# Four-layer graph network on one core: where the transposed adjacency lies in memory, and when the last pair of layer 2 is finished

## The chip, the cores and the metric

The kernel runs on 1 core of one Trainium2 chip, in float32. The time is the device time of one launch in microseconds (us), median over runs. Engines are called as in the profile: PE (TensorE matmul), DVE (VectorE), ACT (ScalarE), POOL (GpSimd) and SP (SyncE, which here only issues DMAs).

## The reference

`x` has 32 batches of 512 nodes and 64 features; `adj` is a 512 by 512 symmetric, normalized adjacency with self edges. Each of four layers adds its result to x:

```python
# layer 0
h = relu(layernorm(x));  x = x + h @ Ws + (adj @ h) @ Wn + bias
# layer 1, twice: z = relu((adj @ z) @ W[i]), from z = h
h = relu(layernorm(x));  x = x + z
# layer 2: graph attention
h = relu(layernorm(x));  Wh = h @ W.T;  e = leaky_relu(e1[:, None] + e2[None, :], 0.2)
x = x + elu(softmax(where(adj > 0, e, -9e15)) @ Wh)
# layer 3: 8 heads and an output attention, each as
#   s = (h h^T) * adj;  s = where(s == 0, -1e16, s);  softmax(s) @ h + b
# heads joined by leaky_relu, then the output attention and leaky_relu, added to x
```

## The kernel before

**Tiling.** Nodes lie on the 128 partitions, four to each (C = 4), and batches are worked on in 16 pairs. x stays in SBUF for the whole launch. Layers 0 to 2 run as a software pipeline over the pairs (`slot(k)`), in which each pair is a few steps behind the one before it. The tail of that pipeline, `drain()`, is an order written out by hand: the string `LAST` names each step and its pair (`exp_15` is the exp of pair 15, the last).

**Layer 3** is a list `flow` of units: 128 head units (two heads of one batch each) and 16 output units. `flow_period(t)` issues period t of a pipeline over units: the scores of unit t (rows r = 2, 3) and of unit t+1 (r = 0, 1), L428 on PE; their maxima (L443 on DVE: one custom instruction that adds the mask, negates and keeps the row maximum; two for each r, as a unit holds two heads); the row maxima go out to DRAM and come back broadcast (`spread_out`, `spread_in`, on SP's queue) into `topb`; unit t-1 has the maximum subtracted (`shift`, L467 and L471, on POOL in most periods; in period 3, EARLY + 1, rows 1 and 3 are on DVE) and the exp (L480 on ACT); rows are joined in pairs (`join`, L483 on DVE), summed (`totals`), and multiplied with the features (`values`, L489 on PE), after which `normalize` (L538 on DVE) writes `o_att` and so frees the `av` bank. The score tiles have two buffers in PSUM (`ps_s`), which the odd rows' exps also use. The first two units are begun within `drain()`, so that layers 2 and 3 overlap; their `topb` lies in the memory of the transposed adjacency `adj_t`, which by then is read no more (L457). Unit 1's four shifts are on POOL.

**The end of a layer 2 pair.** `read` (L1161) forms o; `exp` (L1169, ACT) its exponential; `grow` (L1175, L1176 and the two instructions of `centre`, L919 and L921) adds elu(o) to x, sums the rows and writes the centred x over o; `square` (L1180, ACT) and a sum (L958, DVE) give the variance; `root` (L965, ACT, a square root, for which ACT loads another function table) and `turn` (L973, DVE, a reciprocal) the factor that layer 3's features of that pair need. Those features are used only when layer 3 comes to batches 30 and 31. The last pair's o and e are kept past layer 2: `o_end` and `e_end` take both buffers of the tag `hs3` in the pool `early`, which layer 3 uses for scaled features (`features(2)`, L575). In the kernel before, `end_of_gat` does grow, square, sum, root and turn of the last pair between periods 2 and 3.

**Memory.** Pools are laid one behind the other. Behind what is kept for good comes `setup` (8 KB for each partition for `adj_raw`, later the mask, and some 4.2 KB of small weights), then `adj_t` (8 KB), then the buffers of layers 0 to 2. After layer 2 all of these are given back, and layer 3's pools take their place: `pairs_b`, five buffers of 4 KB for pairs of rows (cat and y), and then `pbuf`, six buffers of 4 KB for `p_att`, where maxima are written. Five times 4 KB is a little less than the 20.5 KB or so of setup and `adj_t`, so that the first `p_att` buffer begins on the last bytes of `adj_t`, which are the second half of unit 1's `topb`. Unit 2's first maxima go into that buffer.

**Order.** In both stages the order of instructions on PE, DVE and ACT is the order of the source (`manual_schedule`); in layer 3 also that of POOL and SP. Waits between engines are put in where memory or data asks for them.

Of the kernel before, what the change touches and what calls it, by code (L numbers as in the profile page):

```python
# [8 lines left out]
F32 = mybir.dt.float32  # L9
# [5 lines left out]
P = 128  # L15
# [7 lines left out]
def fast_form(  # L23
# [26 lines left out]
    B, N, F = x.shape  # L50
    C = N // P
# [20 lines left out]
    early = ctx.enter_context(tc.tile_pool(name="early", bufs=1))  # L72
# [6 lines left out]
    lasting += [  # L79
        adj_p.rearrange("p c k q -> p c (k q)")[:, c : c + 2] for c in range(0, C, 2)  # L80
    ]
    setup_ctx = ExitStack()
    setup = setup_ctx.enter_context(tc.tile_pool(name="setup", bufs=1))
    adj_raw = setup.tile([P, C, N], F32, name="adj_raw", tag="raw")
# [57 lines left out]
    m2 = const.tile([P, H, F], F32, name="m2")  # L142
    bh01 = const.tile([P, H], F32, name="bh01")
    wa1 = setup.tile([P, P], F32, name="wa1")
    adj_t_ctx = ExitStack()
    adj_t_pool = adj_t_ctx.enter_context(tc.tile_pool(name="adjt", bufs=1))
    adj_t = adj_t_pool.tile([P, C, N], F32, name="adj_t")

    adj_f = adj_p.rearrange("p c k q -> p c (k q)")
    flow_neg = const.tile([P, C, N], F32, name="flow_neg")  # L150

# [98 lines left out]
    def row_pair(name):  # L250

        return pairs.tile([P, 2, N], F32, name=name, tag="row")
# [102 lines left out]
    EARLY = 2  # L355
# [429 lines left out]
    def planned(units, products):  # L785

        class Nothing:
            def __getattr__(self, name):
                return lambda *args: None

        nothing = Nothing()

        def period(t):
            def unit(lag):
                return units[t - lag] if 0 <= t - lag < len(units) else nothing


            now, ahead, last = (unit(i) if t - i >= EARLY else nothing for i in (0, -1, 1))
            made = unit(1) if t > 1 else nothing
            summed = unit(2) if t > 2 else nothing  # L800
            for r in range(2, C):
                now.scores(r)
            unit(3).recips_in()
            unit(6).store()
            unit(4).bias()
            last.shift(0, nc.gpsimd)
            made.exps(0)
            summed.totals()
            summed.totals_out(1, nc.scalar)
            u, h = products.get(t - 1, (None, 0))  # L810
            if u and h == H - 1:
                u.keep_product()
            last.shift(2, nc.gpsimd)
            made.exps(2)
            for r in range(2, C):
                now.maxima(r)
            now.spread_out()
            if t == EARLY + 1:
                last.shift(1, nc.vector)
                last.shift(3, nc.vector)  # L820
            summed.totals_out(0, nc.sync)
            now.spread_in()
            for r in range(2):
                ahead.scores(r)
            unit(4).y_pe()
            unit(4).y_act()
            unit(3).normalize()
            for r in range(2):
                ahead.maxima(r)
            unit(4).back()  # L830
            unit(4).y_dve()
            unit(4).back_dve()
            if t != EARLY + 1:
                last.shift(1, nc.gpsimd)
            made.exps(1)
            for j in range(C):
                summed.values(j)
            u, h = products.get(t, (None, 0))
            if u:
                u.product(h)  # L840
            unit(2).recips()
            unit(2).recips_out()
            made.join(1)
            if t != EARLY + 1:
                last.shift(3, nc.gpsimd)
            made.exps(3)
            unit(5).back_pool()
            unit(-2).make_gs()
            made.join(3)
            unit(-3).features(3)  # L850
            unit(-2).judge_product()
            unit(1).make_v()
            unit(-4).make_hx()
            unit(-2).make_g()
            unit(-2).copy_g()
            for step in range(3):
                for lag, odd in ((step - 7, 0), (step - 11, 1)):
                    u = unit(lag)
                    if getattr(u, "i", None) == 0 and u.b % 2 == odd:
                        u.features(step)  # L860
            if t == len(units) + 1:
                any_zero()

        return period
# [21 lines left out]
    assert not due and len(late) == LATE  # L886
    for i, u in enumerate(flow):
        u.at = i
    flow_period = planned(flow, products)


# [8 lines left out]
    with (  # L900
# [110 lines left out]
        class Gat:  # L1011
# [134 lines left out]
            def read(self):  # L1146
                op, den = self.op, self.den
                rec = tiny.tile([P, 2, C], F32, name="rec")
                den = den.rearrange("p (c k e r) -> p k c e r", c=C, k=2, e=2)
                nc.vector.tensor_reduce(rec, den[:, :, :, :, 0], AX.X, OP.add)  # L1150
                nc.vector.reciprocal(rec, rec)

                if self.i == LATEST:
                    self.sq, self.e = (
                        early.tile([P, 2, C, F], F32, name=n, tag="hs3", bufs=2)
                        for n in ("o_end", "e_end")
                    )
                else:
                    self.sq = work.tile([P, 2, C, F], F32, name="o")
                o = self.sq  # L1160
                nc.vector.tensor_tensor(  # L1161
                    o, op.rearrange("p c k f -> p k c f"),
                    rec[:, :, :, None].to_broadcast([P, 2, C, F]), OP.mult,
                )

            def exp(self):
                if self.i != LATEST:
                    self.e = pairs_a.tile([P, 2, C, F], F32, name="e", bufs=1)
                nc.scalar.activation(self.e, self.sq, AF.Exp)  # L1169

# [16 lines left out]
        n0, n1, n2, gat = {}, {}, {}, {}  # L1187
# [126 lines left out]
        LATEST = M - 1  # L1314
# [11 lines left out]
        c_15 wh_15 s0_1 vq_15 read_13 sh0_0 exp_13 acc_14 sh1_0 ex0_0 sh2_0 ex1_0 weigh_15  # L1326
        den_14 kacc_14 sh3_0 ex2_0 op_14 kden_14 sc0_15 s1_1 ex3_0 dps_14 sc1_15 m0_1 m1_1
        s2_1 read_14 s3_1 m2_1 acc_15 m3_1 j1_0 spread_1 den_15 j3_0 kacc_15 rest_13 op_15
        kden_15 dps_15 osq_13 exp_14 ovar_13 read_15 rest_14 exp_15 osq_14 ovar_14
        """  # L1330

        def drain():
# [111 lines left out]
        def keep_stats(sp):  # L1444
            for n in sp.norms:
                if isinstance(n, Gat):
                    flow_stats[n.i] = n.mean, n.rstd

        def end_of_gat(sp):
            gat[LATEST].grow()  # L1450
            gat[LATEST].square()
            sp.add(gat[LATEST])
            sp.root()
            sp.turn()
            keep_stats(sp)
# [6 lines left out]
        with tc.manual_schedule(  # L1462
            engines={
                mybir.EngineType.PE,
                mybir.EngineType.DVE,
                mybir.EngineType.Activation,
            }
        ):
            start()
            begun = {k: [] for k in range(M)}  # L1470
            for k, step in (
                (0, gat_weights), (1, gat_sizes), (1, edges), (2, masks), (2, own_edges),
                (3, flow_weights), (3, roots), (4, roots_row), (4, flow_squares),
                (5, flow_least),
            ):
                begun[k].append(step)
            for c in range(C):
                begun[5 + 2 * c].append(lambda c=c: judge_rows(c))
                begun[6 + 2 * c].append(lambda c=c: count_rows(c))
            begun[5 + 2 * C].append(judge_counts)  # L1480
            begun[6 + 2 * C].append(judge_across)
            for k, some in (
                (10, (-11, -10, -9)), (11, (-8, -7)), (12, (-6, -5)), (13, (-4, -3)),
                (14, (-2, -1)),
            ):
                for t in some:
                    begun[k].append(lambda t=t: flow_period(t))
            for k in range(M):
                slot(k, begun[k])
            unfinished = drain()  # L1490
    adj_t_ctx.close()
    setup_ctx.close()


    pairs = ctx.enter_context(tc.tile_pool(name="pairs_b", bufs=H - 3))
# [9 lines left out]
    with tc.manual_schedule(  # L1505
        engines={
            mybir.EngineType.PE,
            mybir.EngineType.DVE,
            mybir.EngineType.Activation,
            mybir.EngineType.Pool,  # L1510
            mybir.EngineType.SP,
        }
    ):
        flow[0].totals()
        flow[0].totals_out(1, nc.scalar)
        flow[0].totals_out(0, nc.sync)
        flow_period(1)
        for j in range(C):
            flow[0].values(j)
        flow_period(2)  # L1520
        end_of_gat(unfinished)
        flow[9].features(2)
        for k in range(3, len(flow) + ROOM):
            flow_period(k)
# [562 lines left out]
```

## Time and profile before

| what | us |
|---|---|
| median of 3 runs (lowest to highest) | 2010.44 (2010.34 to 2012.5) |
| the profiled execution's own time | 2012.36 |
| its span, first to last instruction | 2010.6 |
| layer 2's last `grow` (L1175 of `o_end`) begins | 448.58 |
| period 2's end to period 3's maxima, DVE | 448.58 to 455.35 |

The span is told in us from its first instruction. "Busy" is time in which an engine executes; a wait is put down to what came last before the waiting instruction could go. PE's clock can be granted in full (1.00) or in part, and the window view tells it for each stretch. Idle time of an engine that nothing waits for costs nothing.

### The profile page before, as it was taken

The numbers are of one execution on the slowest core, as the hardware profiler recorded it, in microseconds if no ns is written. First come the engines' busy times: TensorE is split into PE (matmuls) and PEld (weight loads), VectorE is DVE, ScalarE is ACT, GpSimd is POOL, SyncE is SP. The second block draws the span as 40 slices with busy tenths as digits, with TensorE's granted clock in tenths as the row PEclk, the third lists the DMA queues.
The fourth block names the chain that finished last, engine by engine and source line by source line (L and its number), as shares of the span: only waits on it lengthen the run. The fifth ranks groups of instructions, "written<-read, shape, count | busy, mean of one in ns | idle before, by whom it ended". The sixth has DMA issues, their size and how long they took to land.

```text
span 2010.6 us, 29032 instructions
## 1 busy us (share of the span) xinstructions
PE 1950.3 (97%) x9338; PEld 728.6 (36%) x9338; DVE 1740.0 (87%) x4109; ACT 1322.4 (66%) x2008; POOL 1442.0 (72%) x832
## 2 busy tenths in 40 slices
PE   7999999979999999999999999999999999999996
PEld 4655554423333333333333333333333333333332
DVE  6799986988898898898889898888888888988994
ACT  3455554536777777777676777767777776766674
POOL 2000000027899999989898989899898898888996
PEclk9999999989999999999999999999999999999998
DMA  4000000002223232322233322332232222222323
GB/s 124 1 1 1 1 1 0 12 24 68 79 72 82 77 85 71 86 76 76 80 81 70 86 74 77 80 81 70 78 78 70 76 72 79 76 70 81 76 76 81
DMA packets 185873, 128.03 MB, mean 64 GB/s; under 512 B 124984, under 2 KB 130272, under 8 KB 185584
## 3 DMA queue, kind: packets, MB, share of 16 engines
q1 hardware_dynamic: 166480, 125.30, 23.3%
q10 hardware_dynamic: 18720, 0.59, 0.5%
q8 instruction: 75, 1.23, 0.3%
q14 instruction: 86, 0.70, 0.1%
q0 software_dynamic: 512, 0.20, 0.1%
HBM read 119.48 MB, written 5.37 MB: 62 GB/s over the span
## 4 chain that ended last, share of the span: by engine, by line
PE 78%; POOL 7%; DVE 6%; DMA 5%; ACT 2%; issue 2%; SPq 0%; ACTq 0%; POOLq 0%; DVEq 0%
PE s_ps L428 21%; PE av L489 20%; PE nt_ps L980 8%; PE tot_ps L501 6%; PE y_ps L624 5%; PE gT_ps L669 5%; PE g_ps L601 3%; PE acc L1096 3%; POOL row L467 2%; POOL p_att L467 2%; DMA topb<-top_row 2%; PE po L1002 1%; DVE row L443 1%; PE den L1107 1%; DMA top_row<-top 1%
## 5 line engine op out<-in xcount | busy, mean ns | idle before, releaser
L428 PE MATMUL s_ps<-g,hx 64*128 64x512 f32 x2048 | 521.1, 618 | 19.9 <-DVE top L443 13.2
L467 POOL TENSOR_TENSOR row<-row,topb 128x1024 f32<-128x1024 f32 x182 | 429.9, 2383 | 0.0
L467 POOL TENSOR_TENSOR p_att<-p_att,topb 128x1024 f32<-128x1024 f32 x182 | 429.9, 2384 | 0.0
L443 DVE CUSTOM_DVE_ANT_0 p_att<-s_ps,flow_neg 128x512 f32<-128x512 f32 x492 | 310.4, 687 | 50.0 <-PE s_ps L428 43.4
L443 DVE CUSTOM_DVE_ANT_0 row<-s_ps,flow_neg 128x512 f32<-128x512 f32 x496 | 312.6, 686 | 38.9 <-PE s_ps L428 38.5
L428 PEld LDWEIGHTS s_ps<-g,hx 64*128 64x128 f32 x2048 | 177.2, 187 | 330.0 <-DVE top L443 186.8
L471 POOL TENSOR_TENSOR p_att<-p_att,topb 128x512 f32<-128x512 f32 x124 | 156.2, 1281 | 75.4 <-DMA topb<-top_row 63.6
L1229 POOL TENSOR_TENSOR x<-x,bias_b 128x512 f32<-128x512 f32 x16 | 20.4, 1278 | 255.6 <-DVE hn L921 255.6
L642 DVE SCALAR_TENSOR_TENSOR cat<-y_ps,bh,cat 128x512 f32<-128x512 f32 x256 | 180.1, 746 | 15.1 <-ACT cat L634 13.4
L471 POOL TENSOR_TENSOR row<-row,topb 128x512 f32<-128x512 f32 x120 | 151.0, 1280 | 58.7 <-DMA topb<-top_row 50.9
L618 ACT COPY g<-g_ps 128x512 f32<-128x512 f32 x128 | 131.8, 1138 | 84.8 <-PE g_ps L601 84.8
L634 ACT ACTIVATE cat<-y_ps,bh 128x512 f32<-128x512 f32 x256 | 161.4, 682 | 34.9 <-PE y_ps L624 34.3
L480 ACT ACTIVATE row<-row 128x1024 f32<-128x1024 f32 x126 | 133.4, 1059 | 69.7 <-POOL row L471 35.5
L480 ACT ACTIVATE p_att<-p_att 128x1024 f32<-128x1024 f32 x123 | 130.3, 1060 | 68.1 <-POOL p_att L471 34.1
L483 DVE TENSOR_TENSOR p_att<-e_ps,p_att 128x1024 f32<-128x1024 f32 x123 | 145.3, 1198 | 13.2 <-ACT e_ps L480 12.9
L483 DVE TENSOR_TENSOR row<-e_ps,row 128x1024 f32<-128x1024 f32 x122 | 144.2, 1197 | 13.4 <-ACT e_ps L480 13.2
L480 ACT ACTIVATE e_ps<-p_att 128x1024 f32<-128x1024 f32 x123 | 125.7, 1029 | 34.4 <-POOL p_att L467 28.3
L480 ACT ACTIVATE e_ps<-row 128x1024 f32<-128x1024 f32 x122 | 124.7, 1029 | 31.7 <-POOL row L467 25.0
L467 POOL TENSOR_TENSOR adj_p<-adj_p,topb 128x1024 f32<-128x1024 f32 x60 | 143.1, 2385 | 0.0
L624 PE MATMUL y_ps<-o_att,wh_sb 64*128 64x512 f32 x512 | 136.8, 594 | 0.0
L669 PE MATMUL gT_ps<-cat,wo_sb 128*64 128x512 f32 x512 | 131.6, 592 | 0.0
L980 PE MATMUL nt_ps<-adj_t,hn 128*128 128x512 f32 x256 | 119.0, 609 | 4.8 <-DVE unsound L272 3.0
(239 smaller groups left out, 3442.6 us busy)
## 6 DMA issues: line engine op xcount, KB each, us to landing
topb<-top_row SPq DMA_DIRECT2D x284, 256.0 KB
recb<-rec_row SPq DMA_DIRECT2D x288, 128.0 KB
out_dram<-y SPq DMA_DIRECT2D x32, 128.0 KB
x<-in_x_dram SPq DMA_DIRECT2D x3, 1024.0 KB
top_row<-top SPq DMA_DIRECT2D x144, 4.0 KB
parts<-tot SPq DMA_DIRECT2D x144, 4.0 KB
parts<-tot ACTq DMA_DIRECT2D x144, 4.0 KB
rec_row<-rec_flow SPq DMA_DIRECT2D x144, 4.0 KB
```

Source lines behind the costliest of these rows:

```text
L428: nc.tensor.matmul(ps[k], lhsT=x[halves(k), r * P : (r + 1) * P], rhs=g[halves(k), :], start=True, stop=True,)
L443: nc.vector.tensor_tensor_reduce(out=self.p[r][:, k], in0=ps[k], in1=flow_neg[:, r], scale=-1.0, scalar=BIG, op0=OP.add, op1=OP.min, accum ...
L467: engine.tensor_tensor(self.p[r], self.p[r], self.topb, OP.subtract)
L471: engine.tensor_tensor(p, p, self.topb[:, k], OP.subtract)
L480: nc.scalar.activation(to, self.p[r], AF.Exp, scale=-1.0)
L483: nc.vector.tensor_tensor(self.p[r], self.joined.pop(r), self.p[r - 1], OP.add)
L489: nc.tensor.matmul(self.av[halves(k), :], lhsT=self.v(k, j) if j % 2 else self.less_next(k, j), rhs=self.p[j][:, k], start=(j == 0), stop= ...
L624: nc.tensor.matmul(ps, lhsT=wh_sb[halves(k), 2 * self.i + k, :], rhs=self.o[halves(k), :], start=True, stop=True,)
L634: nc.scalar.activation(self.cat[:, k], self.y[k], AF.Identity, bias=bh01[:, h : h + 1], scale=0.01)
L642: nc.vector.scalar_tensor_tensor(self.cat[:, k], self.y[k], bh[:, h : h + 1], self.cat[:, k], op0=OP.add, op1=OP.max,)
L669: nc.tensor.matmul(self.gps[halves(k), :], lhsT=wo_sb[:, h, :], rhs=Heads.cat.pop((self.b + k, h)), start=(h == 0), stop=(h == H - 1),)
L980: nc.tensor.matmul(p, lhsT=lhs(k), rhs=adj_t[:, k, :], start=(k == 0), stop=(k == C - 1))
```

## The change

Three things are done together.

1. `adj_t` is allocated ahead of `setup` and given back after it. It then lies under the first two of the five row-pair buffers of layer 3, and `setup` under the other three and the first bytes of `pbuf`.
2. The last pair's exp is taken out of `drain()`; `e_end` is no more. Its place is a row-pair buffer, taken in period 3. `o_end` alone takes a buffer of the tag `hs3`, and `features(2)` of unit 9 follows period 2 at once.
3. exp, grow, square and sum of the last pair are issued within period 3, after `copy_g` and ahead of the features; root and turn at the same place of period 5.

```diff
@@ memory @@
+    adj_t_ctx = ExitStack()
+    adj_t_pool = adj_t_ctx.enter_context(tc.tile_pool(name="adjt", bufs=1))
+    adj_t = adj_t_pool.tile([P, C, N], F32, name="adj_t")
     setup_ctx = ExitStack()
     setup = setup_ctx.enter_context(tc.tile_pool(name="setup", bufs=1))
...
-    adj_t_ctx = ExitStack()
-    adj_t_pool = adj_t_ctx.enter_context(tc.tile_pool(name="adjt", bufs=1))
-    adj_t = adj_t_pool.tile([P, C, N], F32, name="adj_t")
@@ period(t) @@
             unit(-2).copy_g()
+            for step in extra.pop(t, ()):
+                step()
             for step in range(3):
@@ Gat.read, Gat.exp @@
-                    self.sq, self.e = (
-                        early.tile([P, 2, C, F], F32, name=n, tag="hs3", bufs=2)
-                        for n in ("o_end", "e_end")
-                    )
+                    self.sq = early.tile([P, 2, C, F], F32, name="o_end", tag="hs3", bufs=2)
...
-                if self.i != LATEST:
+                if self.i == LATEST:
+                    self.e = row_pair("e")[:, 0].rearrange("p (k c f) -> p k c f", k=2, c=C)
+                else:
                     self.e = pairs_a.tile([P, 2, C, F], F32, name="e", bufs=1)
@@ LAST @@
-        kden_15 dps_15 osq_13 exp_14 ovar_13 read_15 rest_14 exp_15 osq_14 ovar_14
+        kden_15 dps_15 osq_13 exp_14 ovar_13 read_15 rest_14 osq_14 ovar_14
@@ end_of_gat @@
         def end_of_gat(sp):
+            gat[LATEST].exp()
             gat[LATEST].grow()
             gat[LATEST].square()
             sp.add(gat[LATEST])
+
+        def last_stats(sp):
             sp.root()
             sp.turn()
             keep_stats(sp)
@@ after drain() @@
             unfinished = drain()
+            extra[EARLY + 1] = [lambda: end_of_gat(unfinished)]
+            extra[EARLY + 3] = [lambda: last_stats(unfinished)]
+    setup_ctx.close()
     adj_t_ctx.close()
-    setup_ctx.close()
@@ layer 3 @@
         flow_period(2)
-        end_of_gat(unfinished)
         flow[9].features(2)
```

More of the change, by code (lines that the diff above doesn't have):

```diff
@@ L888, in fast_form @@
         u.at = i
+    extra = {}
     flow_period = planned(flow, products)
```

## The prediction

> Notation: unit t is the t-th entry of layer 3's list `flow`; s(t,r) its score matmuls (L428), m(t,r) its maxima (L443, two instructions of 0.61 us start to start), shift, exp, join the steps that follow. All times are us on the trace's axis; "before" times are read, "after" times are worked out.
>
> **What bounds the kernel now.** First the busy shares and the chain that ended last, then the chain in order of time at the passage from layer 2 to layer 3, then that passage's waits, timeline and clock.
>
> ```profile
> PE 1950.3 (97%) x9338; PEld 728.6 (36%) x9338; DVE 1740.0 (87%) x4109; ACT 1322.4 (66%) x2008; POOL 1442.0 (72%) x832
> ...
> PE 78%; POOL 7%; DVE 6%; DMA 5%; ACT 2%; issue 2%; SPq 0%; ACTq 0%; POOLq 0%; DVEq 0%
> ```
>
> PE is the bound: what it loses is lost (in the window view of 477.7 to 488.5, one period, PE is busy 10.8 of 10.8 us, DVE 9.75). The change touches only the passage, where the chain leaves PE:
>
> ```profile
> 434.25 2.31 POOL adj_p L467
> 436.55 0.02 issue
> 436.58 0.69 DVE p_att L443
> ...
> 448.67 0.61 DVE x L1175
> ...
> 455.13 0.05 DVE rstd L973
> ...
> 460.84 4.35 PE av L489 x16
> 465.19 1.92 PE s_ps L428 x8
> ```
>
> From 460.84 on the chain is PE without a gap for 156 us. Two holes lie before it. m(2,0) could start at 430.44 (its scores ended at 429.4), but waits for POOL's last shift of unit 1, which reads the bytes of `adj_t` under the first `p_att` buffer:
>
> ```profile
> DVE p_att L443 <- POOL adj_p L467: 6.1, 1, 6.1
> ```
>
> And from 448.58 to 455.35 (6.8 us) DVE works off the last pair's end, root and turn. Now DVE and POOL side by side:
>
> ```profile
> 428.14 1.57 DVE L1176 SCALAR_TENSOR_TENSOR x<-e,x 128x512 f32<-128x512 f32 x1
> ...
> 429.13 2.80 POOL L467 TENSOR_TENSOR adj_p<-adj_p,adj_t 128x1024 f32<-128x1024 f32 x1
> 431.90 2.35 POOL L467 TENSOR_TENSOR row<-row,adj_t 128x1024 f32<-128x1024 f32 x1
> ...
> 449.30 0.69 DVE L1176 SCALAR_TENSOR_TENSOR x<-e_end,x 128x512 f32<-128x512 f32 x1
> ...
> 450.75 2.07 DVE L921 SCALAR_TENSOR_TENSOR o_end<-sum,x 128x256 f32<-128x256 f32 x2
> ...
> 453.49 1.28 ACT L965 ACT_TABLE_LOAD   x1
> 454.79 0.32 ACT L965 ACTIVATE std<-var,eps 128x24 f32<-128x24 f32 x1
> ```
>
> The same L1176 takes 0.69 with POOL idle and 1.57 with POOL at work. Last the clock (columns: stretch, its length, busy us of PE, PEld, DVE, ACT, POOL, granted clock, then the DMAs' share and GB/s):
>
> ```profile
> 445.20:448.60 3.40, 1.44 (x6) 0.30 (x4) 3.37 (x9) 3.17 (x4) 0.00 (x0) 1.00 0.20 65
> 448.60:452.00 3.40, 3.40 (x14) 0.70 (x12) 3.30 (x6) 1.43 (x5) 2.24 (x2) 0.51 0.30 104
> ...
> 455.50:458.90 3.40, 2.25 (x6) 1.13 (x8) 3.40 (x10) 3.37 (x6) 0.00 (x0) 0.50 0.04 1
> 458.90:462.30 3.40, 3.00 (x8) 0.58 (x6) 3.40 (x8) 1.62 (x3) 0.00 (x0) 0.50 0.30 59
> ```
>
> After a stretch with PE little used the clock is 0.5, and a stretch with PE busy 2.25 of 3.40 did not bring it back; one with 3.00 did.
>
> **The change part by part.** No DMA is added, dropped or moved; the order on PE, POOL and SP is the same. Moved are one exp (ACT 0.63), the end (DVE x, x, sum, o, o; ACT square; DVE var) from ahead of m(3,2) to ahead of m(4,2), and root (ACT) with turn (DVE) to ahead of m(6,2), with two table loads.
>
> *The rule that decides.* Row: 1.57 against 0.69 above. The Trainium skill, "SBUF — State Buffer", section "Who interferes with whom": a DVE instruction with two SBUF inputs and a POOL instruction that reads SBUF share a port as an exclusive lock; one waits for the whole of the other. The trace agrees in detail: x<-e was held until POOL's instruction ended at 429.17 and ended at 429.71, and POOL's next took 2.80 in place of 2.35; of the two o_end, POOL went between them. So they take turns. x, o and DVE's shift have two SBUF inputs; m, join, sum and var have not. With quiet durations the sum is -8; with turns it is +3.6. I take turns, because three rows show them.
>
> 1. *POOL wait goes.* m(2,0)'s first half starts at 430.44, not 436.58. But next on DVE are the two o of pair 14, which before ran at 437.19 with POOL idle. Now POOL's shifts are under way: the first o waits to 431.93, POOL's next (2.2 after a handover) to 434.43, the second o to 434.7. m(2,0)'s second half: 434.63 against 437.87. Gain 3.2 of the 6.1. PE, no longer idle for a whole stretch, now runs s(2,2) at full clock (1.17 to the result; 2.13 before), so m(3,1) ends at 442.2 against 446.1, and unit 1's joins, which wait for ACT's exps, at 445.0 against 448.67: lead 3.7.
>
> 2. *End, root, turn leave.* m(3,2) follows the join: 445.15 against 455.35. s(3,3) issues only at 445.05, when I expect the clock at 0.5 (PE's stretch before has some 1.2 of 3.4): result after 2. m(3,3) ends at 448.3 against 457.8: lead 9.5.
>
> 3. *DVE's two shifts of unit 2.* Before: 2.35 us from 457.74, with POOL idle. Now POOL is in the same unit: from m(2,3)'s end to POOL's first shift it was 6.2 (443.58 to 449.76), so 439.7 + 6.2 = 445.9, and DVE asks in the middle, at 448.3. In turns: DVE to 449.45, POOL to 451.7, DVE to 452.75; the o_att that follows ends at 453.35 against 460.69. Lead 7.3; 2.1 given back. PE's av starts at 453.5.
>
> 4. *The end in its new place.* From o_att to unit 2's joins 5.0, as before: 458.3 against 465.69. On DVE then x, x, sum, o, o, var. Quiet: 0.72 + 0.72 + 0.73 + 0.76 + 0.65 (square) + 0.69 = 4.3. But POOL shifts unit 3: m(3,3)'s end to POOL's start was 6.0; 0.3 more, because SP's `parts` of unit 1 goes first and waits for a copy behind ACT's exp: 454.6. Its instructions end at 455.9, 457.1, 459.45. x to 460.0, POOL to 462.2, x to 462.75, POOL to 464.95, o to 465.25, o to 465.65, square to 466.3, var to 467.05. Cost 8.7. m(4,2) starts at 467.0; before 466.30. Queued behind it on DVE are all later maxima; PE's s(5,0) waits for its score buffer. On ACT, the new exp is over at 457.6 (hidden by the joins); the square blocks the `hs` copies (1.26; their buffer is freed by var), an exp and the `tot` copy, which ends at 470.0, 1.2 later than before; y_ps needs it only at 472, so that is hidden while PE is late, and would cost some 0.2 if it were not.
>
> 5. *PE after the hole.* s(5,0) can start at 468.3, against 468.04, but PE has been idle since 460.3, so the clock is 0.5. The clock view changes at 455.5, 458.9, 462.3, every 3.4; on that grid come 465.7, 469.1, 472.5, and only the stretch to 472.5 is full. In the before kernel s, s, y took 2.8 from there; at half clock until 472.5 they do 2.1 of it and end at 473.2 against 470.85. PE is 2.3 late.
>
> 6. *Root and turn.* In period 5 ACT copies hx until 487.99 (before axis), then load 1.28, std 0.32, turn at 489.65, m(6,2) at 489.87 against 488.48: 1.4 later. DVE had 0.97 us idle there, waiting for PE; PE's s(7,0) and s(7,1) wait for m(6,2) and m(6,3), so PE loses 1.3. The second load (1.28) delays exp and copies of unit 5 by 2.4, falling to 0.9 at the last e_ps, whose join comes later still: hidden by DVE's own delay. Here a second rule speaks against the change: "ScalarE: Activation LUTs", section "What ACT_TABLE_LOAD costs", gives 1.28 and a drain of 1.38 with every switch, which would make the loss 2.7. The trace shows no such drain: square ends at 453.47, load at 453.49, std at 454.79. I take 1.3 and keep 2.7 as the far end.
>
> The buffer of `e` in the row pairs (five deep) shifts the turn of cat and y by one; each waits for the one five back as before: nothing, and at most one exp's wait.
>
> Sum: +2.3 + 1.3 = +3.6. On the profiled execution that is a span of 2010.6 + 3.6 = 2014.2. Its own time was 2012.36, the span and 1.8 around it; the median of the runs shown is 1.9 lower, 2010.44, so I forecast 2014.0. 0.2% is 4.0 us, about what a measurement of this kernel can tell from no change.
>
> **The rivals.**
>
> *Faster: the turns cost little.* If DVE's instructions get in at their quiet durations, av starts at 447.7, unit 2's joins end at 452.7, var at 456.9, and m(4,2) leads by 9.4; less the root 1.3 this is -8: 2002.4. For it: 13 us of named waiting do leave the chain. Against: the 1.57 and 2.07 rows. If turns are spared only in step 4, it is -3 (2007.5). 0.17 together.
>
> *Slower: the clock stays low for a further stretch.* PE restarts at 468.3 in a hole of 8 us. The stretch that begins at about 469.1 must be nearly full to bring the clock back; with 2.25 of 3.40 it did not. If s(5,0) starts after about 469.8, which is m(4,2) 1.5 later than I work out (one turn of POOL, 2.35, is enough), half clock lasts to 475.9: y ends near 475.6, 4.8 late, with the root +6: 2016.5. For it: where the stretches fall against the work is chance. Against: step 4 hangs on one landing, and I have put that late already. 0.22.
>
> *It doesn't do what it says:* the first `p_att` may lie over something else still in use. The waits of the new program name only its scores. That, or gains and losses that cancel near 2010: 0.06.
>
> **How the numbers follow.** Likeliest case 0.55: 2014.0, alone 2012 to 2016, of which 0.36 within 0.2% and 0.19 above. Slower rival 0.22, faster rival 0.17 (0.15 by over 0.2%), cancelling 0.06. Faster 0.15, same 0.36 + 0.02 + 0.06 = 0.44, slower 0.41. The range leaves out the deep end of the faster rival and the drain on top of the slower: 2007 to 2017.
>
> **What would show it.** Right: no POOL wait at m(2,0); the two o of pair 14 at 2 us or more apart; DVE shifts of unit 2 some 4.4 long together; POOL instructions of 2.8 between x and x; var 8 to 9 us after the joins; clock 0.5 around 469; av of unit 1 near 453.5; a load before m(6,2). Wrong: x, x at 0.69 in period 3 with POOL at work, or PE's s(5,0) before 465.

## The result, and the profile after

The changed kernel takes 2016.56 us (median of 9 runs, 2014.36 to 2019.60); the kernel before, run beside it, 2010.88 (9 runs, 2008.62 to 2013.62). The ratio is 1.0027, 95% interval 1.0017 to 1.0036: slower by 5.5 us or so. The profiled execution of the changed kernel took 2016.66 us and its span is 2014.8.

The page first: shares of engines, and the chain by engine.

```profile
PE 1949.0 (97%) x9338; PEld 728.5 (36%) x9338; DVE 1750.7 (87%) x4109; ACT 1320.6 (66%) x2008; POOL 1443.6 (72%) x832
...
PE 77%; POOL 8%; DVE 7%; DMA 4%; ACT 3%; issue 2%; SPq 0%; ACTq 0%; POOLq 0%; DVEq 0%
```

DVE issues as many instructions as before (x4109) and is busy 10.7 us longer. Nothing was added to it; some of its instructions have become longer. The chain in order of time (start, length, what) says which:

```profile
424.84 1.71 DVE x L1176
...
426.65 2.67 DVE x L1177
...
429.94 0.68 DVE p_att L442
...
430.63 3.65 DVE o L923 x2
434.29 0.60 DVE p_att L442
...
434.95 3.92 PE s_ps L427 x8
...
457.96 1.38 DVE x L1176
...
459.44 2.67 DVE x L1177
...
462.85 4.22 DVE o_end L923 x2
...
469.77 3.78 PE s_ps L427 x8
```

L442 is the maxima (L443 before), L427 the scores, L923 the two o. The wait of m(2,0) for POOL is gone: it starts at 429.94. But the two o of pair 14 now run between its two halves and take 3.7 us; the last pair's x and o in period 3 take 1.4, 2.7 and 4.2. POOL over the same times, in the timeline:

```profile
423.50 2.50 POOL L470 TENSOR_TENSOR row<-row,adj_t 128x512 f32<-128x512 f32 x2 [106.47 <-DMA adj_t<-top_row]
...
425.95 2.81 POOL L466 TENSOR_TENSOR adj_p<-adj_p,adj_t 128x1024 f32<-128x1024 f32 x1
428.72 2.81 POOL L466 TENSOR_TENSOR row<-row,adj_t 128x1024 f32<-128x1024 f32 x1
...
458.74 2.81 POOL L466 TENSOR_TENSOR row<-row,topb 128x1024 f32<-128x1024 f32 x1
461.51 2.79 POOL L466 TENSOR_TENSOR p_att<-p_att,topb 128x1024 f32<-128x1024 f32 x1
464.26 2.52 POOL L466 TENSOR_TENSOR row<-row,topb 128x1024 f32<-128x1024 f32 x1
```

Each of the last pair's x ends some 0.55 us behind the end of one of POOL's instructions (459.33 behind 458.79, 462.10 behind 461.55), the last o 0.27 us behind one (467.05 behind 466.78), and POOL's own instructions take 2.8 us, not 2.35: the two engines take turns, one instruction each. The root in period 5, and the clock over period 3's hole (columns as before: stretch, length, busy us of PE, PEld, DVE, ACT, POOL, granted clock):

```profile
491.68 1.28 ACT L967 ACT_TABLE_LOAD   x1
492.97 0.32 ACT L967 ACTIVATE std<-var,eps 128x24 f32<-128x24 f32 x1
...
493.32 0.30 DVE L975 RECIPROCAL rstd<-std 128x24 f32<-128x24 f32 x1 [2.15 <-ACT std L967]
```

```profile
460.00:463.45 3.45, 0.29 (x4) 0.00 (x0) 3.38 (x3) 0.00 (x0) 3.45 (x2) 1.00 0.00 0
463.45:466.85 3.40, 0.00 (x0) 0.00 (x0) 3.40 (x2) 0.00 (x0) 3.32 (x2) 0.50 0.00 0
466.85:470.25 3.40, 0.48 (x2) 0.48 (x4) 2.65 (x9) 2.35 (x6) 0.00 (x0) 0.50 0.00 0
470.25:473.70 3.45, 3.45 (x10) 1.33 (x10) 2.70 (x10) 2.03 (x3) 0.00 (x0) 0.50 0.08 4
473.70:477.10 3.40, 3.40 (x16) 0.92 (x14) 2.97 (x9) 2.52 (x4) 0.60 (x1) 1.00 0.53 154
```

**A common origin.** Runs of one kernel lie up to 5 us apart here (8 in some of the experiments), and the two profiled executions reach the passage at different times: POOL's first shift of unit 1 starts at 426.22 before and at 423.50 after. The 2.7 us lie ahead of the first thing that the change moves. All comparisons of traces below count from that shift, which is called zero.

| from zero, us | before | after | lead after | lead predicted |
|---|---|---|---|---|
| m(2,0), second half | 11.65 | 10.71 | 0.94 | 3.2 |
| unit 1's joins end | 22.44 | 21.79 | 0.65 | 3.7 |
| m(3,3) ends | 31.59 | 24.41 | 7.18 | 9.5 |
| o_att ends | 34.47 | 28.38 | 6.09 | 7.3 |
| unit 2's joins end | 39.47 | 34.46 | 5.01 | 7.4 |
| m(4,2) | 40.08 | 44.91 | -4.83 | -0.7 |
| m(5,2) | 51.53 | 57.91 | -6.38 | -2.3 |
| m(6,2) | 62.25 | 70.04 | -7.79 | -3.6 |
| end of span | 1584.36 | 1591.28 | -6.92 | -3.6 |

The medians differ by 5.7, the spans of the two profiled executions by 4.2, and counted from zero the change loses 6.9.

### The profile page after: what moved, and what is told of

Its sections match the earlier page's. It is cut to its first block, busy times and chain, and to the rows that moved or that the text cites. A ratio compares the mean times of both kernels' runs of the same rounds, so it can differ in the third digit from the quotient of the medians.

```text
span 2014.8 us, 29037 instructions
## 1 busy us (share of the span) xinstructions
PE 1949.0 (97%) x9338; PEld 728.5 (36%) x9338; DVE 1750.7 (87%) x4109; ACT 1320.6 (66%) x2008; POOL 1443.6 (72%) x832
## 4 chain that ended last, share of the span: by engine, by line
PE 77%; POOL 8%; DVE 7%; DMA 4%; ACT 3%; issue 2%; SPq 0%; ACTq 0%; POOLq 0%; DVEq 0%
PE s_ps L427 21%; PE av L488 20%; PE nt_ps L982 8%; PE tot_ps L500 5%; PE y_ps L623 5%; PE gT_ps L668 5%; POOL p_att L466 3%; PE g_ps L600 3%; PE acc L1098 3%; POOL row L466 2%; DMA topb<-top_row 2%; DVE p_att L442 2%; PE po L1004 1%; PE den L1109 1%; POOL p_att L470 1%
## 5 line engine op out<-in xcount | busy, mean ns | idle before, releaser
L427 PE MATMUL s_ps<-g,hx 64*128 64x512 f32 x2048 | 522.4, 619 | 23.5 <-DVE top L442 17.8
L442 DVE CUSTOM_DVE_ANT_0 p_att<-s_ps,flow_neg 128x512 f32<-128x512 f32 x492 | 310.1, 685 | 43.9 <-PE s_ps L427 43.5
L442 DVE CUSTOM_DVE_ANT_0 row<-s_ps,flow_neg 128x512 f32<-128x512 f32 x496 | 312.5, 685 | 37.9 <-PE s_ps L427 37.2
L427 PEld LDWEIGHTS s_ps<-g,hx 64*128 64x128 f32 x2048 | 177.3, 187 | 334.3 <-DVE top L442 191.1
```

The costliest lines, as they stand in the source:

```text
L427: nc.tensor.matmul(ps[k], lhsT=x[halves(k), r * P : (r + 1) * P], rhs=g[halves(k), :], start=True, stop=True,)
L442: nc.vector.tensor_tensor_reduce(out=self.p[r][:, k], in0=ps[k], in1=flow_neg[:, r], scale=-1.0, scalar=BIG, op0=OP.add, op1=OP.min, accum ...
```

## The experiments

The theory that they test: the change loses by DVE's turns behind POOL (the two o of pair 14, and the end in period 3), by half clock behind PE's hole, and by the root. The rivals: the new place in memory costs, or the clock does, or DVE has no room for the work. Ratios are to the kernel before, run beside each; chips differ by some 4 us, so ratios are compared and not times.

**1 and 2. Each part alone.** The memory part alone (the end stays between periods 2 and 3):

```diff
+    adj_t = adj_t_pool.tile(...)          # ahead of setup, closed behind it
     setup_ctx = ExitStack()
```

> Only the memory part of the change: the transposed adjacency lies under the row pairs; exp, end, root and turn of the last pair stay where they were before the change. Theory (steps 1 of the prediction alone): the POOL wait of 6.1 us at m(2,0) goes, the two o of pair 14 give back 2.9 of it, so unit 1's joins, the end, m(3,2) and PE's av all come 3 to 4 us earlier: about 2007.2 us, 3.7 below the kernel before. Rival A (the port or the clock takes the rest of it too): 2010 to 2012. Rival B (the new place itself costs, for instance through a buffer that comes free later): 2014 or more, that is most of what the whole change lost.

Measured: 2008.14 us (22 runs, 2005.52 to 2013.82), ratio 0.9988 (0.9981 to 0.9994): 2.4 below the kernel before, so the memory part gains. The interval stands for 1.2 to 3.8 us, so that the theory's 3.7 lies at its edge. Its profiled execution, at the slow end with 2013.30, shows what can take the gain. Timeline, DVE and then POOL:

```profile
448.07 0.68 DVE L1174 SCALAR_TENSOR_TENSOR x<-o_end,x 128x512 f32<-128x512 f32 x1
448.79 1.65 DVE L1175 SCALAR_TENSOR_TENSOR x<-e_end,x 128x512 f32<-128x512 f32 x1
...
451.19 3.13 DVE L920 SCALAR_TENSOR_TENSOR o_end<-sum,x 128x256 f32<-128x256 f32 x2
```

```profile
448.54 3.02 POOL L470 TENSOR_TENSOR p_att<-p_att,topb 128x512 f32<-128x512 f32 x2 [12.61 <-PE s_ps L427]
```

POOL's shifts of unit 2 have moved up beside the end, which takes 8.7 us from join to m(3,2) where it took 6.7.

The deferral alone:

```diff
-    adj_t ahead of setup
+    adj_t in its old place                # all else as in the changed kernel
```

> Only the deferral: exp and end in period 3, root and turn in period 5; the transposed adjacency lies where it lay before. Theory (the deferral is what loses, and the memory part gains 3 to 4): m(2,0) waits 6.1 us for POOL again, and the time is 3 to 4 us above the changed kernel, 2020. Rival A (POOL's turns and PE's clock in period 3 swallow whatever lead there was): the same as the changed kernel, 2016.6. Rival B (the memory part is what loses): 2011 to 2013.

Measured: 2018.86, ratio 1.0039 (1.0027 to 1.0052). The deferral loses by itself; whether it loses more than the whole change, the intervals don't tell. The trace has the reason for so small a difference:

```profile
436.05 0.69 DVE L442 CUSTOM_DVE_ANT_0 p_att<-s_ps,flow_neg 128x512 f32<-128x512 f32 x1 [6.13 <-POOL adj_p L466]
436.67 0.76 DVE L923 SCALAR_TENSOR_TENSOR o<-sum,x 128x256 f32<-128x256 f32 x2
```

While m(2,0) waits for POOL, POOL runs out of work, and the two o behind it take 0.76. Without the wait they take 3.7. m(3,1) ends 19.96 from zero here, 19.90 in the kernel before and 19.24 in the changed kernel: the wait of 6.1 us was exchanged for turns, and 0.7 us is what is left of it.

**3. The end left out.** exp, x, x, sum, o, o, square and variance of the last pair are dropped.

> The changed kernel with the last pair's exp, x, x, sum, o, o, square and variance left out (layer 3 gets pair 14's mean and factor in its place, so the last pair's result is not the reference's); root and turn stay in period 5. Theory (the end costs 10.5 us of DVE time in period 3 by waiting its turn behind POOL, and PE waits for all of it beyond its hole): m(4,2) follows unit 2's joins at once, 10.4 us earlier, PE's hole of 9.5 us shrinks to under 1, and the time falls by 8 to 9.5, to 2007 to 2008.5. Rival (PE's half clock after earlier holes is the main loss, the end only fills a hole that is there anyway): the time falls by 4 or less, 2012.5 or more.

Measured: 2006.13, ratio 0.9977 (0.9968 to 0.9987), 0.0050 below the changed kernel, that is 10 us. PE's hole of 9.5 us is gone; s(5,0) follows `totals` at once. So the end's cost in period 3 is no cover for a hole that is there anyway.

**4. Turn two periods after the root.**

```diff
-            extra[EARLY + 3] = [lambda: last_stats(unfinished)]
+            extra[EARLY + 3] = [unfinished.root]
+            extra[EARLY + 5] = [lambda: last_stats(unfinished)]   # turn alone
```

> The changed kernel with the turn (DVE's reciprocal) two periods after the root (ACT) in place of the same period; the table loads stay in period 5. Theory (the root costs only because DVE stands still for ACT's table load, 2.15 us before the reciprocal): 1.4 us below the changed kernel, 2015.2. Rival (the two table loads delay ACT's exps and so PE, wherever the turn stands): no change, 2016.6.

Measured: 2019.11 (5 runs, 2013.78 to 2020.05), ratio 1.0034 (1.0021 to 1.0047): the intervals overlap, so the time doesn't settle it. In the trace, m(5,2) to m(7,2) takes 22.30 us; before the change it was 21.71, after it 23.05. The stop before the reciprocal is gone, but `cat` then waits 0.66 for ACT, which is late by its loads. About half of the 1.3 us comes back.

**5. The same end, spread over places where POOL is idle.** e gets a buffer of its own in layer 3 (2 KB for each partition), so that o_end's buffer is free after the first x and the exp.

```diff
             unit(4).y_dve()
+            for step in quiet.pop(t, ()):
+                step()
...
+            quiet[EARLY + 1] = [grow_o];      extra[EARLY + 1] = [last.exp]
+            quiet[EARLY + 2] = [grow_e]
+            quiet[EARLY + 3] = [centre_last]; extra[EARLY + 3] = [last.square]
+            quiet[EARLY + 4] = [lambda: unfinished.add(last)]
+            extra[EARLY + 5] = [unfinished.root]
+            quiet[EARLY + 7] = [lambda: last_stats(unfinished)]
```

> The changed kernel with the last pair's end spread out: the first x in period 3, the second in period 4, sum with the two o and the square in period 5, the variance in period 6, each behind y's DVE step, where the trace of the changed kernel shows POOL idle for 2.6 to 3.7 us before its next shifts; root in period 7, turn in period 9; e has a buffer of its own. The same work is done as in the changed kernel. Theory (the end costs by its turns behind POOL): x, x at 0.69 us each and the o at about 0.4 each, m(4,2) follows unit 2's joins at once, no root wait, PE's hole ahead of s(5,0) under 1 us: 10 to 11 us below the changed kernel, 2005 to 2007, about where the kernel without the end stood (2006.1), less 1.4 for the root. Rival (DVE has no room for 4.3 us of work in periods 3 to 6, PE waits for it there): 2009 to 2013.

Measured: 2005.96, ratio 0.9977 (0.9970 to 0.9985), the same as with the end left out. The timeline of its DVE, in periods 3, 4 and 5:

```profile
454.70 0.68 DVE L1455 SCALAR_TENSOR_TENSOR x<-o_end,x 128x512 f32<-128x512 f32 x1
...
465.75 1.05 DVE L1460 SCALAR_TENSOR_TENSOR x<-e_end,x 128x512 f32<-128x512 f32 x1
...
477.91 0.76 DVE L925 SCALAR_TENSOR_TENSOR e_end<-sum,x 128x256 f32<-128x256 f32 x2
```

0.68, 1.05 (it met the tail of a shift that ended at 466.25) and 0.76, against 1.45, 2.66 and 4.20. The instructions are the same, and what POOL does meanwhile differs: the three rows take 8.31 us in the changed kernel; with POOL idle throughout they take 0.69, 0.69 and 0.76, together 2.14. So 6.2 of the 10.45 us that the end takes there ahead of m(4,2) are turns. The other 4.3, the prediction's quiet sum, are the end's own time in that place. Spreading takes that away too, as most of it now falls into DVE's waits for PE (ahead of m(5,2) DVE waits 2.17 us in the changed kernel and 1.05 here). The 10 us of this run are therefore not turns alone: by the lengths, turns are the larger part and the place the smaller. Two more things differ: e has its own buffer, and root and turn stand apart, which is worth 1.4 us at most (term 6 below). No run keeps the end whole ahead of m(4,2) with POOL idle. That DVE has no room for the work is ruled out, since the work is all there.

**6 and 8. Pair 14 ahead.** In the order of layer 2's tail, pair 14's exp and its whole x, x, sum, o, o go ahead of the read of pair 15, alone (6) and with the spread end (8).

```diff
-        kacc_15 rest_13 op_15 kden_15 dps_15 osq_13 exp_14 ovar_13 read_15 rest_14 osq_14 ovar_14
+        kacc_15 rest_13 exp_14 op_15 kden_15 dps_15 osq_13 rest_14 ovar_13 osq_14 read_15 ovar_14
```

> The changed kernel with one more edit in the hand-written order of layer 2's tail: pair 14's exp ahead of pair 13's square, and pair 14's x, x, sum, o, o ahead of pair 13's variance and of the read of pair 15. Theory (m(2,0)'s second half comes late because the x and o of pair 14 each wait for a shift of POOL): they run before POOL's first shift or between its two short ones, m(2,0) and m(2,1) follow their scores without the 4.3 us between the first and the second half, PE's hole of 4.4 us goes or falls under 2, and m(3,1) ends 3 us or more earlier counted from POOL's first shift of unit 1: 3 to 5 us below the changed kernel, 2012 to 2013.5. Rival (the lead is lost again in period 3, where DVE then meets POOL at another place): within 1.5 us of the changed kernel, 2015 to 2018.

> Both together: the end spread out over periods 3 to 6 with root and turn apart, and pair 14's x, x, sum, o, o early. Theory (both are turns behind POOL in different places, so the gains add): 2001 to 2004, which would be 7 to 9 us below the kernel before. Rival (PE is bound by then and the second gain is swallowed): 2005 to 2007, as with the spread end alone.

Measured: 2018.15, ratio 1.0037 (1.0024 to 1.0050), and 2007.27, ratio 0.9978 (0.9969 to 0.9988): nothing gained, the expectation was wrong. A new wait stands in the place of the old; PE's timeline of run 6:

```profile
428.41 2.08 PE L427 MATMUL s_ps<-g,hx 64*128 64x512 f32 x4 [4.52 <-DVE o_end L1160]
```

s(2,0) is written to the PSUM bank that the read of pair 15 (L1160) frees, and that read now starts 3.91 us from zero in place of 0.65.

**9. Only pair 14's x, x ahead of the read; sum, o, o behind it**, with the spread end:

```diff
+        kacc_15 rest_13 exp_14 op_15 kden_15 dps_15 osq_13 gx_14 read_15 cen_14 ovar_13 osq_14 ovar_14
```

> The kernel with the spread end, and in layer 2's tail pair 14's exp ahead of pair 13's square and only its x, x ahead of the read of pair 15; sum, o, o stay behind that read, which so goes 3.6 us earlier than with the whole of pair 14's end ahead of it. Theory (the read of pair 15 frees the PSUM bank in which s(2,0) is written, and every two-SBUF-input instruction taken out of POOL's shifts is worth one turn): x, x at 0.69 us each, s(2,0) by 425.5 as in the changed kernel, m(2,0)'s second half 2 to 4 us earlier counted from POOL's first shift of unit 1, PE's hole ahead of s(2,2) under 2 us: 2 to 4 us below the spread end alone, 2002 to 2004. Rival (what is won there is lost again in the turns of period 3's shifts): 2005 to 2006.5, as the spread end alone.

Measured: 2006.65 where the kernel before took 2014.67 on that chip, ratio 0.9962 (0.9950 to 0.9975): the lowest ratio of all, some 8 us below the kernel before. The intervals of this run and run 5 overlap, so the times don't show that it is better than run 5; the traces show what moved. DVE, then PE:

```profile
424.93 0.69 DVE L1178 SCALAR_TENSOR_TENSOR x<-o,x 128x512 f32<-128x512 f32 x1
425.72 0.69 DVE L1179 SCALAR_TENSOR_TENSOR x<-e,x 128x512 f32<-128x512 f32 x1
...
428.15 3.39 DVE L925 SCALAR_TENSOR_TENSOR o<-sum,x 128x256 f32<-128x256 f32 x2
```

```profile
434.00 2.35 PE L427 MATMUL s_ps<-g,hx 64*128 64x512 f32 x8 [0.76 <-DVE top L442]
```

The two x are quiet, the two o still take turns, PE's hole ahead of s(2,2) is 0.76 in place of 4.39, and m(3,1) ends 13.99 from zero in place of 19.24. Part of it was lost again in period 3, as the rival had it: m(4,2) is at 32.25 against 35.19 in run 5, so 5.4 us of lead over run 5 have become 2.9, and 0.9 at the end of these two executions (1578.4 and 1579.4 from zero).

**7 and 10. PE kept busy in the hole** with 20, then 9 matmuls that nobody reads, on the changed kernel:

```diff
+            if t == EARLY + 2:
+                for _ in range(n):
+                    nc.tensor.matmul(warm_ps, lhsT=ident, rhs=flow_neg[:, 0], start=True, stop=True)
             for r in range(2):
                 ahead.scores(r)
```

> The changed kernel with 20 matmuls on PE whose result nobody reads, in period 4 ahead of s(5,0): they fill 8.6 of the 9.5 us in which PE is idle there. Theory (half clock after the hole costs 1.55 us of the 6.9): the clock stays 1.00 through the hole, s(5,0) to m(5,2) take 11.45 us from m(4,2) as before the change in place of 13.0, and the time is 1.5 us below the changed kernel, 2015. Rival A (the clock is the larger part of the loss): 4 us or more below. Rival B (the fillers run at half clock themselves or stand in the way): at or above 2016.6.

> The changed kernel with 9 unread matmuls on PE in period 4 ahead of s(5,0), of 0.86 us each as the run with 20 of them measured, so 7.7 us in a hole of 9.5. Theory (half clock behind the hole costs 1.55 us): clock 1.00 from there on, 11.45 us from m(4,2) to m(5,2) in place of 13.0; about 2015, 1.5 below the changed kernel. Rival A (the clock is the larger part of the loss): 2012.5 or less. Rival B (no effect): 2016.6.

Run 7 was mis-sized (each matmul takes 0.86 us, not 0.43): the fillers ran to 483.3, 13 us past m(4,2), and the time was 2022.31, ratio 1.0055 (1.0042 to 1.0069). Run 10: 2017.53, ratio 1.0014 (1.0006 to 1.0022), so 0.0013 below the changed kernel, with intervals that just overlap. Its clock and PE:

```profile
463.00:466.40 3.40, 3.40 (x11) 1.44 (x8) 3.33 (x3) 0.00 (x0) 3.40 (x2) 1.00 0.00 0
466.40:469.80 3.40, 3.40 (x9) 1.52 (x8) 2.64 (x6) 1.69 (x5) 0.24 (x1) 1.00 0.00 0
469.80:473.30 3.50, 3.50 (x14) 1.46 (x14) 2.85 (x10) 2.69 (x4) 0.00 (x0) 1.00 0.08 3
```

```profile
471.22 1.99 PE L427 MATMUL s_ps<-g,hx 64*128 64x512 f32 x8
473.04 1.02 PE L623 MATMUL y_ps<-o_att,wh_sb 64*128 64x512 f32 x4
```

From s(5,0) to y 1.82 us at full clock, 3.57 without the fillers: half clock behind the hole costs 1.75. The fillers still ended 1.3 us after s(5,0) could have gone, so m(4,2) to m(5,2) fell from 13.0 to 12.3 only.

**11. o_att between DVE's two shifts of period 3**, on run 9's kernel:

```diff
                 last.shift(1, nc.vector)
+                unit(3).normalize()
                 last.shift(3, nc.vector)
```

> The kernel with the spread end and the split pair 14, and o_att of unit 0 between DVE's two shifts of unit 2 in period 3, in place of behind both. Theory (the shifts' turns of 2.1 us hold o_att and with it PE's av; with the end out of the way PE is bound from there): av starts 1.5 to 2 us earlier and PE gains up to 1.5: 0.5 to 1.5 us below the kernel without this edit. Rival (unit 2's joins come 0.7 later and take it back): no difference.

Measured: 2008.28, ratio 0.9966 (0.9954 to 0.9978), no difference to run 9. av starts 23.34 from zero in place of 25.79, but then PE stands idle for 3.56 us until unit 2's joins, and s(4,2) runs at half clock: an earlier av only moved the hole.

**12. Run 9's kernel with the transposed adjacency in its old place.**

> The kernel with the spread end and the split pair 14 (ratio 0.9962 to the kernel before), with the transposed adjacency back in its old place, so that this is the kernel before plus the two moves of work. Theory (the memory part is worth what it moves ahead at m(2,0), once nothing behind it gives that back): m(2,0) waits for POOL's last shift of unit 1 again, 4 us later than without, and the ratio is 0.998, some 3.5 to 4 us above the kernel without this edit. Rival (the wait at m(2,0) lies beside other waits): no difference, 0.996.

Measured: 2011.29 where the kernel before took 2014.41, ratio 0.9991 (0.9983 to 0.9999), 0.0029 above run 9. The wait is back:

```profile
434.20 0.69 DVE L442 CUSTOM_DVE_ANT_0 p_att<-s_ps,flow_neg 128x512 f32<-128x512 f32 x1 [3.95 <-POOL adj_p L466]
```

The two intervals don't overlap. So the memory part is worth some 5 us (4.6 by the medians against the kernel before, 5.8 by the ratios) once nothing behind it gives that back; in run 1 it gained 2.4, and with the changed kernel's end behind it more than half of it was hidden.

## Why the prediction was right or wrong

The time came out inside the stated range, 0.4 us below its upper end; the likeliest case had 2.6 us too little. The forecast had given 0.41 to "slower by over 0.2%" and 0.44 to "within 0.2%"; measured are 0.27%, with an interval (0.17 to 0.36) that reaches to both sides of that line. The mechanism, turns behind POOL, was right; three terms of the sum (1, 3 and 4 below) were mis-sized. Counted from zero the loss was 6.9 where 3.6 was forecast. The range reached up to 2017 on account of the slow rival, whose mechanism did not occur, so that the time lies inside it is in part luck. Term by term, counted from zero (the gain or loss between two rows of the table):

1. *POOL's wait at m(2,0)* was to give 3.7 at unit 1's joins and gave 0.65. The mechanism was right: the wait went and the two o of pair 14 fell into POOL's shifts. The count of turns was short by one. I took the two x of pair 14 over from the trace before, where the first was issued at 427.25, 0.20 us ahead of POOL's second shift, and went in front of it (0.80 us). In the changed kernel it was issued at 424.76, 0.03 us behind that shift's start at 424.73, and had to wait it out (1.78); the second x then waited for the third shift (2.66), and both o came one shift later. And PE, whose hole was to close, was idle for 4.39 and ran s(2,2) at half clock, not full. This differs by execution: in run 10, whose program is the same up to there, the x was issued 0.01 us ahead of POOL's second shift (427.70, 427.71) and took 0.68. m(2,0)'s second half then stands at 8.49 from zero, where the prediction works out to 8.41, and the lead at unit 1's joins is 3.04.
2. *End, root and turn leave*: gain 6.5 from joins to m(3,3); 5.8 was predicted, since the clock stayed full in that stretch.
3. *DVE's shifts in turns with POOL*: 1.1 lost, 2.2 predicted. They took 3.44 us together where some 4.4 were forecast (runs 2, 7 and 10: 4.57 to 5.08), because DVE got in one turn earlier. Term 4 has the price of that.
4. *The end in its new place*: the largest loss, and mis-sized in two places. From o_att to the joins 1.1 more than the 5.0 taken over from before, as unit 2's exps now wait for POOL's lengthened shifts (3.49 and 3.35). The end itself took 10.45 from the joins to m(4,2), 8.7 predicted. Three waits for POOL were forecast (x, x and the first o), with the last o 0.4 behind the first; four were measured, as the last o waited for one more shift. Of the six profiled executions with the end in period 3, three (runs 2, 7 and 10) took 8.5 to 8.7 and three (the changed kernel, runs 4 and 6) 10.4 to 10.6; one more shift of POOL is worth 1.9 us. The traces show where it comes from. Lines from the changed kernel's timeline, POOL, DVE and ACT:

```profile
446.70 3.49 POOL L470 TENSOR_TENSOR p_att<-p_att,topb 128x512 f32<-128x512 f32 x2 [12.70 <-PE s_ps L427]
447.84 3.44 DVE L466 TENSOR_TENSOR p_att<-p_att,topb 128x1024 f32<-128x1024 f32 x2
450.16 3.35 POOL L466 TENSOR_TENSOR p_att<-p_att,topb 128x1024 f32<-128x1024 f32 x1
450.23 1.06 ACT L479 ACTIVATE p_att<-p_att 128x1024 f32<-128x1024 f32 x1 [2.42 <-POOL p_att L470]
...
456.28 2.51 POOL L470 TENSOR_TENSOR p_att<-p_att,topb 128x512 f32<-128x512 f32 x2 [2.36 <-DMA topb<-top_row]
```

   DVE asked 1.14 us after POOL's start (runs 4 and 6: 1.13, 1.12), while POOL was still in the first of its two short shifts, and went between the two, so that the pair took 3.49 in place of 2.50. ACT's exp waits for that pair, the `tot` copy (451.19) comes behind the exp, SP's `parts` (451.78, for which SP waited 2.9 us) behind the copy, and behind `parts` on SP's queue comes the `topb` that POOL waits for at 456.28. So POOL began unit 3's shifts 8.4 us after m(3,3)'s end (runs 4 and 6: 8.5, 8.3), where the prediction had 6.3. The end's first x met POOL's first shifts 1.6 us after their start, not 3.7, and one more shift lay ahead of the last o. In runs 2, 7 and 10 DVE asked 1.8 to 2.3 us after POOL's start, the pair took 2.50 to 2.52, POOL began unit 3 after 6.3 to 6.95, x came 3.55 to 3.7 us behind that, and the end took the 8.5 to 8.7 of the forecast. The prediction thus describes this second order of turns. From m(3,3)'s end to m(4,2) it takes 18.6 to 19.3 us, the first order 20.4 to 20.6. What decides which of the two an execution gets I have not traced.
5. *PE after the hole*: 1.55 lost between m(4,2) and m(5,2), 1.6 predicted; run 10 gives 1.75 by itself.
6. *Root and turn*: 1.41 lost, 1.3 predicted. std starts 0.01 us after the load ends, and the load 0.03 after ACT's copy: the drain of 1.38 that the Trainium skill, "ScalarE: Activation LUTs", section "What ACT_TABLE_LOAD costs", gives with every switch is not in this trace either, as it was not in the one before, and the measurement decides.

Between m(6,2) and the end 0.9 came back in ways that I have not traced. The sum is -6.9 where -3.6 was predicted; that the span differs by only 4.2 is the 2.7 by which this execution reached the passage earlier.

The slow rival had the time almost to the digit (2016.5), and that is luck. Its mechanism, half clock for a further 3.4 us behind s(5,0), is not in the trace: the clock came back at 473.70, one stretch after s(5,0) began. What made the kernel slow was the turn that this rival named only as its trigger. The faster rival's claim, that turns cost little, fell with the lengths: 1.45, 2.66 and 4.20 in turns, 0.69, 0.69 and 0.76 with POOL idle.

## What to carry to other kernels

Before moving an instruction into "free" time of its engine, look at what the engine that it takes turns with (here POOL) does at that moment: count turns, not durations, and give the count an error of one turn at each end, because 0.04 us in the arrival of one instruction decided such a turn here (run 10 against the changed kernel). A wait that is removed lets the instructions behind it run into what the wait had kept them from; here 6.1 us of waiting for POOL became turns with POOL, and the maxima behind them, m(3,1), end only 0.7 us earlier (19.24 from zero, 19.90 before). Deferred work pays when it is cut up and put one piece at a time where the other engine is known to wait (here behind y, while POOL waits for its DMA), and when the piece that frees a buffer for the next stage stays in front.

## What the runs showed of the hardware that was not expected

POOL pays for turns too. A shift of 2.35 to 2.38 us takes 2.8 when a DVE instruction waits for its turn, 0.45 more. That is close to the 0.6 us or so for which the DVE instruction ahead of it still ran after the shift's start (the x that ends at 462.10, the shift that starts at 461.51), so it may be nothing but POOL's own wait; no run separates the two. POOL's pair of 128x512 shifts took 3.49 in place of 2.50 where one DVE shift went between them, and the shift behind it 3.35 in place of 2.36 where the other did; that is how DVE's turns delayed ACT's exps.

How long PE was busy in one stretch does not by itself tell which clock the next one gets. In these traces, on their 3.4-us grid and at full clock, stretches with PE busy 0.29, 0.91, 1.18 and 1.26 us were followed by 0.50 or 0.51, one with 2.14 was not. In between the traces disagree: 1.44 was followed by 0.50 (run 9), 1.73 was not (run 1), and the kernel before has both, 1.44 followed by 0.51 (its stretch of 445.20, shown with the prediction) and 1.45 followed by full clock:

```profile
438.80:442.20 3.40, 1.44 (x8) 0.42 (x6) 3.37 (x10) 2.88 (x4) 0.00 (x0) 1.00 0.14 24
442.20:445.60 3.40, 3.40 (x12) 0.81 (x12) 2.43 (x6) 3.11 (x10) 1.18 (x1) 0.50 0.47 134
```

```profile
431.60:435.00 3.40, 1.45 (x8) 0.28 (x4) 0.00 (x0) 0.00 (x0) 3.40 (x3) 1.00 0.01 2
435.00:438.40 3.40, 0.00 (x0) 0.00 (x0) 1.82 (x5) 0.36 (x1) 1.54 (x1) 1.00 0.00 0
```

```profile
442.95:446.35 3.40, 2.14 (x8) 0.60 (x8) 3.30 (x6) 3.40 (x7) 0.00 (x0) 1.00 0.43 153
446.35:449.80 3.45, 3.03 (x18) 0.84 (x16) 3.45 (x8) 1.46 (x6) 3.10 (x2) 1.00 0.26 79
```

(The first pair is from run 9, the second from the kernel before, the third from the changed kernel.) At half clock, stretches with 2.33 (run 11) and 2.71 (run 1, from 437.90) did not bring full clock back; those with 3.00 (before) and 3.40 did. What else enters is not shown. Where the half-clock stretches fall differs between executions (412.3 in the changed kernel's, 414.5 in the one before, both ahead of the change); part of the 5 us by which runs differ may come from there, which no run here isolates.
